# Two adaLN layers on one core: the transposes of the causal values in four halves, and a later start for the rows to be routed

## The chip, the cores and the metric

The kernel runs on one core of a Trainium2 chip. The metric is the device time of one execution in microseconds (us); the time of a kernel is the median of its runs.

## The reference, cut to what matters

32 sequences of 256 tokens with 128 features pass through two layers. Each layer is attention and then a feed-forward part, each behind a layer norm whose scale and shift, and whose gate at the output, come from a small conditioning matrix. Layer 0 has full attention and a feed-forward part quantized to FP4. Layer 1 has causal attention with 16 heads of 8 features, and a mixture of experts of which each token takes two. The part in question is the causal attention:

```python
qkv = jnp.einsum('bse,ef->bsf', inputs, qkv_kernel) + qkv_bias
qkv_heads = qkv.reshape(b, heads, s, -1)
q, k, v = jnp.split(qkv_heads, 3, axis=-1)
qk = jnp.einsum('bhse,bhte->bhst', q, k) / np.sqrt(2.0 * hidden)
mask = jnp.triu(jnp.full((s, s), -jnp.inf, dtype=jnp.float32), k=1)
attn = jax.nn.softmax(qk + mask, axis=-1)
out = jnp.einsum('bhst,bhte->bhse', attn, v).reshape(b, s, e)
...
x = x + ga * out                      # then layer norm, router, two experts a token
```

## The kernel before

The tokens are handled in 16 groups of 512 (two sequences). Three stages follow each other: layer 0 (all groups), the causal stage, and the expert stage, which takes tiles of 256 or 128 rows that share a pair of experts.

**The causal stage** is one long loop. One turn of it is a *unit*; eight units, numbered 0 to 7, are here called a *pass*, and pass g makes the scores of group g. In each unit:

- `maxima` (L852) makes a part of the scores (matmuls of L866 into `c_s`), adds the mask (L873), and VectorE takes the maxima of it (`c_mx`, L877);
- `values` (L943) multiplies the probabilities made two units earlier with the transposed values (`c_po`, L953);
- `probs` (L916) makes scores of 12 units earlier again, transposed (`c_t`, L925); ScalarE takes their exponentials, two instructions of 128x640 (`c_p`, L933), and GpSimd clears what is above the diagonal (L936).

Between these stand the pieces of a table (`put`, L1265): a piece with place n, slot 0 or 1 and a lead is issued in unit n, before (`k` = 0) or after (`k` = 1) `probs`, for the group that is `lead` after the pass's own. The order of instructions on TensorE (PE), VectorE (DVE), ScalarE (ACT) and GpSimd (POOL) is the order of this program text, since the loop stands in `tc.manual_schedule` (L1311). The transfers that SyncE issues (SP) are put in order by a planner.

**The score banks.** `maxima` and `probs` each take two tiles per unit from one pool of three tiles:

```python
ps_s = ph.enter_context(tc.tile_pool(name="c_ps_s", bufs=3, space=PSUM))
```

Each tile is two PSUM banks of 128x512. A tile can be written again only when the engine that reads it is done: DVE for scores (L877), ACT for `c_t` (L933). The matmuls of L866 go to the first tile for two of the four lanes and to the second for the other two, so a unit's first four weight loads on PE belong to the first tile, the other twelve begin with the second.

Two further pieces borrow a tile of this pool: `d_logits` in unit 4 (router logits of an earlier group, `d_pl`, copied out by ACT at L1052 and L1053), and `c_v` (L842). `c_v` transposes the values of half a group with eight matmuls (`c_pv`, L849), and ACT copies all 128x1024 out to `c_vT` (L850). It stands in slot 1 of units 1 and 5.

Other pieces that the prediction speaks of: `c_turn` (unit 7, slot 0) turns the normalized tokens of a later group (`c_xt`), and ACT writes them modulated to `c_hT`; `d_turn` does the same in unit 1 (`d_hT`); `c_norm` and `d_norm` are the ACT instructions of L782. `d_rank` (L1085 to L1090) and `d_count` are steps of the routing on DVE and PE; they run once for a batch of three groups, in passes 7, 10, 13 and 8, 11, 14.

**Maxima back into q.** `place_maxima` (L902, unit 1) writes the maxima of the group before by eight SP transfers (L912) into `c_q`, from which `c_t` is made from unit 4 on.

**Rows to be routed.** `d_start` (L1000, units 2 and 3, lead -3) takes the moments for the second layer norm. In unit 2 it also takes a tile of `rows` from a pool of six, writes the token numbers (GpSimd iota, L1005) and loads the gates (two SP transfers, L1010). `d_keep` (L1015, unit 4, slot 1) copies the residual into the tile. `d_scatter` (L1160) writes the tiles to DRAM by indirect transfers from GpSimd (L1166); a tile of `rows` is free again when they have landed.

Of the kernel before, what the change touches and what calls it, by code (L numbers as in the profile page):

```python
# [10 lines left out]
F32 = mybir.dt.float32  # L11
BF16 = mybir.dt.bfloat16
I32 = mybir.dt.int32
# [6 lines left out]
P = 128  # L20
D = 128
TPG = 4
GT = TPG * P
# [11 lines left out]
def adaln_two_layers(ctx: ExitStack, tc: tile.TileContext, ins, out: bass.AP):  # L35
    nc = tc.nc
# [21 lines left out]
    TOKEN, WEIGHT, RES, GATE, ROW = D, D + 1, D + 3, 2 * D + 3, 3 * D + 3  # L58
# [36 lines left out]
    xg = []  # L95
# [31 lines left out]
    ident = const.tile([P, P], F32, tag="ident", name="ident")  # L127
# [6 lines left out]
    for l in range(2):  # L134
        sc = mp.tile([NB, D], F32, tag=f"sc{l}", name=f"sc{l}")
        nc.scalar.activation(sc, c_sb[l], AF.Silu)
        pt = mps.tile([P, 512], F32, tag="mps", name=f"mps_t{l}")
# [12 lines left out]
        m = const.tile([D, 6, NB], F32, tag=f"mod{l}", name=f"mod{l}")  # L150
# [81 lines left out]
    with ExitStack() as ph:  # L232
# [12 lines left out]
        sb4 = ph.enter_context(tc.tile_pool(name="ab_sb4", bufs=4))  # L245
        ps = ph.enter_context(tc.tile_pool(name="ab_ps", bufs=3, space=PSUM))
        ps_s = ph.enter_context(tc.tile_pool(name="a_ps_s", bufs=2, space=PSUM))
# [395 lines left out]
    r_rows = ctx.enter_context(tc.tile_pool(name="r_rows", bufs=6))  # L643
# [11 lines left out]
    with ExitStack() as ph:  # L655
# [3 lines left out]
        sb4 = ph.enter_context(tc.tile_pool(name="c_sb4", bufs=4))  # L659
        sb5 = ph.enter_context(tc.tile_pool(name="c_sb5", bufs=5))  # L660
        ps = r_ps
        ps_s = ph.enter_context(tc.tile_pool(name="c_ps_s", bufs=3, space=PSUM))
# [21 lines left out]
        for n in range(NP):  # L684
# [5 lines left out]
            pattern=[[1, P]], channel_multiplier=-1,  # L690
# [6 lines left out]
        gates = {}  # L697
# [10 lines left out]
        L = 32  # L708
        HR = L // 2
        B = 64  # L710
        NQ = NPOS // B
# [52 lines left out]
        def moments_half(m, g, tag, h):  # L764

            x = xg[g]
            if h == 0:
                m["mv"] = ln.tile([P, TPG, 2], F32, tag=f"mv{tag}", name=f"mv{tag}{g}")
            st = ln.tile([P, 2, 6], F32, tag=f"st{tag}", name=f"st{tag}{g}_{h}")
            for i in range(2):  # L770
                nc.vector.bn_stats(st[:, i, :], x[:, 2 * h + i, :])
            for i in range(2):
                nc.vector.bn_aggr(m["mv"][:, 2 * h + i, :], st[:, i, :])
            if h == 1:
                m["stats"] = scales(m.pop("mv"), g, tag)
# [63 lines left out]
            for h in range(2):  # L839
                nc.scalar.activation(vx[:, :, h], m["v", j], AF.Copy, scale=half[:, h : h + 1])  # L840

        def c_v(g, j):  # L842

            m = made[g]
            vT = m["vT", j] = sb4.tile([P, 2 * NQ, 4, L], F32, tag="vT", name=f"c_vT{g}_{j}")
            vx = m["vx", j].rearrange("p n h -> p (n h)")
            pt = ps_s.tile([P, 2, 512], F32, tag="s", name=f"c_pv{g}_{j}").rearrange("p e n -> p (e n)")
            for b in range(2 * NQ):
                nc.tensor.transpose(pt[:, b * P : (b + 1) * P], vx[:, b * P : (b + 1) * P], ident)  # L849
            nc.scalar.copy(vT.rearrange("p j l c -> p (j l c)"), pt)  # L850

        def maxima(u):  # L852

# [141 lines left out]
        toward, batch_of = {}, {}  # L995
# [4 lines left out]
        def d_start(g, h):  # L1000
            m = toward.setdefault(g, {})
            moments_half(m, g, "d", h)
            if h == 0:
                rows = m["rows"] = r_rows.tile([P, TPG, ROW], F32, tag="rows", name=f"d_rows{g}")
                nc.gpsimd.iota(  # L1005
                    rows[:, :, TOKEN : TOKEN + 1].bitcast(I32), pattern=[[P, TPG], [0, 1]], base=g * GT,
                    channel_multiplier=1,
                )
                for h in range(2):
                    nc.sync.dma_start(  # L1010
                        rows[:, 2 * h : 2 * h + 2, GATE : GATE + D],
                        gates[5][2 * g + h : 2 * g + h + 1, :].unsqueeze(1).to_broadcast([P, 2, D]),
                    )

        def d_keep(g):  # L1015
            nc.gpsimd.tensor_copy(toward[g]["rows"][:, :, RES : RES + D], xg[g])

        def d_norm(g, h):
            scaled_half(toward[g], g, "d", h)
# [170 lines left out]
        def row_const(name, shape, values):  # L1190
# [11 lines left out]
            number, pattern=[[1, NMOST]], base=0, channel_multiplier=0, allow_small_or_imprecise_dtypes=True  # L1202
# [62 lines left out]
        def put(n, k, lead, piece, *more):  # L1265
            beside[n][k].append((lead, piece, more))
# [5 lines left out]
        for j in range(NB2):  # L1272
            for n, k, piece, more in (
                (5, 0, c_rows, (0,)), (6, 1, c_apart_q, ()), (6, 0, c_rows, (1,)), (9, 1, c_apart_k, (0,)), (10, 1, c_apart_k, (1,)),
                (7, 0, c_rows, (2,)), (8, 1, c_apart_v, ()), (9, 1, c_v, ()),
            ):
                n += 4 * j
                put(n % NU, k, 1 - n // NU, piece, j, *more)
# [4 lines left out]
        for h in range(2):  # L1283
            put(4 + 4 * h if h == 0 else 0, 0, 3 - h, c_start, h)
            put(1 + 2 * h, 1, 2, c_norm, h)
            put(2 + h, 0, -3, d_start, h)
            put(5 + 2 * h, 1, -3, d_norm, h)
        put(4, 1, -3, d_keep)
        put(1, 0, -4, d_turn)
        put(4, 0, -4, d_logits, 0)  # L1290
# [52 lines left out]
    with ExitStack() as ph:  # L1343
# [3 lines left out]
        sb4 = ph.enter_context(tc.tile_pool(name="d_sb4", bufs=4))  # L1347
# [7 lines left out]
        for c in range(NCH):  # L1355
            lo, hi, here = c * P, (c + 1) * P, []
            while lo < hi:
                e = lo // HID1
# [165 lines left out]
```

## Time and profile before

| | |
|---|---|
| three runs | 1520.52, 1524.13 (median), 1525.28 us |
| the profiled execution | 1523.4 us, span 1521.7 us, mean granted TensorE clock 0.969 |
| busy over the span | PE 92%, DVE 65%, ACT 51%, POOL 49% |
| 0 to 415 us, layer 0 | PE busy 342.0 us, clock 0.94 |
| 415 to 467 us, causal stage before and at the first exponentials | PE 46.1 of 52 us, clock 0.85 |
| 467 to 920 us, causal stage, even run | PE 439.6, DVE 370.8, ACT 309.8, POOL 287.0 of 453 us, clock 1.00 |
| 920 to 976 us, its end and the first expert tile | PE 36.9 of 56 us, clock 0.86 |
| 976 to 1522 us, expert tiles | PE 530.5 of 546 us, clock 0.99 |

The views name an instruction by its line and by output and input tile. PE is the matmul itself, PEld its weight load; a row of the timeline is a run of equal instructions (x16) with its start, its length, and in brackets the engine's idle time before it and who ended that. fp32 matmuls appear twice each, so the eight matmuls of one unit's L866 are x16. A busy PE also contains waits within a run of matmuls, so the PEld rows tell more precisely when PE was held.

### The profile page before, as it was taken

To read this page: it belongs to the slowest core of one execution; us is meant where nothing else is said; L and a number is where in the kernel's file an instruction comes from. 1 tells how busy PE (TensorE), PEld (TensorE's weight loads), DVE (VectorE), ACT (ScalarE), POOL (GpSimd) and SP (SyncE) were. 2 spreads that over 40 slices of the span, in tenths; PEclk is the share of its full clock that TensorE was granted. 3 is DMA by queue.
4 is the path that set the end of the run, shared out by engine and by line. 5 is a ranking of instruction groups with operands and counts; after the bars stand their busy time and mean duration, and the time that the engine had idled before them with its cause. 6 is when DMAs were issued, how large, how long until landed. Compare 5 with 4: busy or idle time off the path is not lost.

```text
span 1521.7 us, 33348 instructions
## 1 busy us (share of the span) xinstructions
PE 1395.0 (92%) x12505; PEld 1097.1 (72%) x12505; DVE 995.9 (65%) x2219; ACT 770.7 (51%) x1491; POOL 743.9 (49%) x1079
## 2 busy tenths in 40 slices
PE   5888989988689999999999999598999999999997
PEld 4665666644357677767677676487999999999996
DVE  6799998999487887888887877146333333333332
ACT  5998877843345677667667657241222222222221
POOL 4767866674334555558668577426222222122122
PEclk9999999998799999999999999799999999999999
DMA  8000000000000000001102011866657777777760
GB/s 225 1 1 1 1 1 1 1 1 1 12 2 3 13 17 14 20 6 58 38 26 67 14 44 55 268 178 210 192 170 238 232 218 227 228 216 232 230 188 11
DMA packets 132065, 139.25 MB, mean 92 GB/s; under 512 B 14377, under 2 KB 105969, under 8 KB 131905
## 3 DMA queue, kind: packets, MB, share of 16 engines
q1 hardware_dynamic: 125600, 119.92, 27.1%
q0 software_dynamic: 6304, 17.21, 3.1%
q8 instruction: 99, 1.62, 0.5%
q14 instruction: 62, 0.50, 0.1%
HBM read 116.95 MB, written 19.61 MB: 90 GB/s over the span
## 4 chain that ended last, share of the span: by engine, by line
PE 73%; DVE 16%; ACT 3%; issue 3%; POOL 3%; DMA 1%; SPq 1%; POOLq 0%; DVEq 0%; ACTq 0%
PE d_y L1439 12%; PE d_pg L1453 11%; PE d_pu L1453 11%; PE c_t L925 8%; PE c_s L866 7%; PE c_po L953 5%; PE c_pq L803 3%; PE c_s L873 2%; PE c_pv L849 2%; DVE c_mx L877 2%; PE b_pu L485 2%; DVE qxh L382 2%; DVE sch L378 1%; DVE sch L370 1%; PE b_pg L476 1%
## 5 line engine op out<-in xcount | busy, mean ns | idle before, releaser
L1459 DVE TENSOR_TENSOR d_h<-d_act,d_pu 128x512 f32<-128x512 f32 (+2 forms) x207 | 132.9, 643 | 298.9 <-PE d_pu L1453 273.0
L1457 ACT ACTIVATE d_act<-d_pg 128x512 f32<-128x512 f32 (+2 forms) x207 | 116.2, 561 | 401.7 <-PE d_pg L1453 353.7
L877 DVE TENSOR_REDUCE c_mx<-c_s 128x10 f32<-128x640 f32 x256 | 198.5, 817 | 68.5 <-PE c_s L873 67.3
L933 ACT ACTIVATE c_p<-c_t 128x640 f32<-128x640 f32 x256 | 166.1, 701 | 120.2 <-PE c_t L925 116.9
L1439 PE MATMUL d_y<-d_wd,d_h 128*128 128x128 f32 (+1 forms) x1656 | 209.4, 281 | 5.5 <-DVE d_h L1459 2.9
L1439 PEld LDWEIGHTS d_y<-d_wd,d_h 128*128 128x128 f32 (+1 forms) x1656 | 198.7, 191 | 20.9 <-DVE d_h L1459 7.0
L1453 PE MATMUL d_pg<-d_sT,d_wg 128*128 128x256 f32 (+1 forms) x924 | 204.3, 348 | 1.2 <-DMA d_wg<-in_L_ffn_w_dram 1.2
L1453 PE MATMUL d_pu<-d_sT,d_wu 128*128 128x256 f32 (+1 forms) x924 | 200.9, 344 | 0.5 <-DMA d_wu<-in_L_ffn_w_dram 0.5
L936 POOL TENSOR_SCALAR_AFFINE_SELECT c_p<-c_p 128x256 f32<-128x256 f32 x256 | 111.4, 442 | 145.7 <-ACT c_p L933 144.3
L1453 PEld LDWEIGHTS d_pu<-d_sT,d_wu 128*128 128x128 f32 x924 | 154.6, 192 | 17.0 <-DMA d_wu<-in_L_ffn_w_dram 1.2
L866 PEld LDWEIGHTS c_s<-c_k,c_qx 32*128 32x128 f32 x2048 | 106.7, 188 | 68.3 <-issue 24.0
L866 PE MATMUL c_s<-c_k,c_qx 32*128 32x256 f32 (+3 forms) x2048 | 141.5, 335 | 12.1 <-ACT c_p L933 8.8
L1453 PEld LDWEIGHTS d_pg<-d_sT,d_wg 128*128 128x128 f32 x924 | 142.1, 193 | 13.0 <-DVE d_sT L1422 1.6
L1478 POOL TENSOR_TENSOR d_o<-d_o,d_slot 128x256 f32<-128x256 f32 (+1 forms) x42 | 25.3, 604 | 244.7 <-DVE d_o L1477 234.8
L925 PE MATMUL c_t<-c_q,c_kx 32*128 32x128 f32 (+3 forms) x2048 | 139.2, 332 | 4.3 <-DVE c_mx L877 3.4
L1481 POOL DMA_INDIRECT out_dram<-d_o,d_slot x69 | 68.5, 993 | 141.5 <-DMA out_dram<-d_o,d_slot 129.0
L925 PEld LDWEIGHTS c_t<-c_q,c_kx 32*128 32x128 f32 x2048 | 111.3, 185 | 28.7 <-DVE c_mx L877 9.1
L953 PE MATMUL c_po<-c_p,c_vT 128*32 128x256 f32 (+3 forms) x2048 | 99.0, 307 | 6.8 <-POOL c_p L936 5.7
L834 POOL TENSOR_SCALAR c_kx<-c_k,half 128x512 f32<-128x512 f32 x64 | 102.4, 1602 | 1.1 <-DVE c_k L819 1.1
L953 PEld LDWEIGHTS c_po<-c_p,c_vT 128*32 128x32 f32 x2048 | 54.6, 109 | 37.0 <-POOL c_p L936 7.6
L485 PE MATMUL b_pu<-wupT,b_hqT 128*128 128x352 f32 x128 | 55.6, 519 | 19.6 <-DVE b_hh L491 19.6
L1166 POOL DMA_INDIRECT slots<-d_rows,d_index x64 | 64.5, 1008 | 16.3 <-issue 15.2
(301 smaller groups left out, 2566.7 us busy)
## 6 DMA issues: line engine op xcount, KB each, us to landing
d_wg<-in_L_ffn_w_dram SPq DMA_DIRECT2D x84, 352.0 KB, 3.5
d_wu<-in_L_ffn_w_dram SPq DMA_DIRECT2D x84, 352.0 KB, 5.3
d_wd<-in_L_ffn_w_dram SPq DMA_DIRECT2D x84, 320.0 KB, 6.2
d_slot<-slots SPq DMA_DIRECT2D x27, 387.0 KB, 3.2
x<-in_L_attn_X_dram SPq DMA_DIRECT2D x16, 256.0 KB, 5.7
d_rows<-gates SPq DMA_DIRECT2D x32, 128.0 KB, 4.7
d_slot<-slots SPq DMA_DIRECT2D x15, 193.5 KB
d_wd<-in_L_ffn_w_dram SPq DMA_DIRECT2D x84, 32.0 KB, 5.8
```

Source lines behind the costliest of these rows:

```text
L485: nc.tensor.matmul(pu[:, :HID0], lhsT=hT[:, i * P : (i + 1) * P], rhs=wT["up"], start=True, stop=True)
L834: nc.gpsimd.tensor_scalar(m["kx", j][:, :, h], m["k", j], half[:, h : h + 1], None, ALU.mult)
L866: nc.tensor.matmul(s[lane // 2][:, lane % 2, at : at + w], lhsT=qx[rows, NQ * e + b, :, :].rearrange("p h n -> p (h n)"), rhs=k[rows, e * ...
L877: nc.vector.tensor_reduce(mx[:, n, 2 * x : 2 * x + 2, :], s[x][:, :, 0:W].rearrange("p l (b n) -> p l b n", n=B), AX.X, ALU.max, negate=True,)
L925: nc.tensor.matmul(s[lane // 2][:, lane % 2, at : at + w], lhsT=kx[rows, (NQ * e + b) * P : (NQ * e + b + 1) * P], rhs=q[rows, (e + 1) * N ...
L933: nc.scalar.activation(t[:, :, 0:W], s[x][:, :, 0:W], AF.Exp, scale=SCALE1)
L936: nc.gpsimd.affine_select(out=diagonal, in_=diagonal, compare_op=ALU.is_ge, fill=0.0, base=1, pattern=[[0, 4], [2, B]] if sub else [[0, 2] ...
L953: nc.tensor.matmul(po[rows, (e + 1) * NPOS - w : (e + 1) * NPOS], lhsT=v[:, NQ * e + b, lane, :], rhs=p[lane // 2][:, lane % 2, at : at + ...
L1439: nc.tensor.matmul(y[k][:, b, :], lhsT=h[r0:r1, j, b * P : (b + 1) * P], rhs=wd[r0:r1, c, :], start=first and b == 0, stop=last and b == N ...
L1453: nc.tensor.matmul(to[:, j, :], lhsT=w[:, c * P : (c + 1) * P], rhs=hT, start=True, stop=True)
L1457: nc.scalar.activation(act[:, :m, :], pg[:, :m, :], AF.Silu)
L1459: nc.vector.tensor_tensor(h[:, :m, :], act[:, :m, :], pu[:, :m, :], ALU.mult)
```

## The change

`c_v` is called four times instead of two: with `e` 0 and 1 for each half of a group, in slot 1 of units 1, 3, 5 and 7. Each call takes a tile of the score banks, uses one of its two banks for four transposes, and ACT copies 128x512 of it. The tile of `rows`, its iota and its two gate transfers move from `d_start` (unit 2) to `d_keep` (unit 4).

```diff
-        def c_v(g, j):
+        def c_v(g, j, e):
             m = made[g]
-            vT = m["vT", j] = sb4.tile([P, 2 * NQ, 4, L], F32, tag="vT", name=f"c_vT{g}_{j}")
+            if e == 0:
+                m["vT", j] = sb4.tile([P, 2 * NQ, 4, L], F32, tag="vT", name=f"c_vT{g}_{j}")
             vx = m["vx", j].rearrange("p n h -> p (n h)")
-            pt = ps_s.tile([P, 2, 512], F32, tag="s", name=f"c_pv{g}_{j}").rearrange("p e n -> p (e n)")
-            for b in range(2 * NQ):
-                nc.tensor.transpose(pt[:, b * P : (b + 1) * P], vx[:, b * P : (b + 1) * P], ident)
-            nc.scalar.copy(vT.rearrange("p j l c -> p (j l c)"), pt)
+            pt = ps_s.tile([P, 2, 512], F32, tag="s", name=f"c_pv{g}_{j}_{e}")[:, 0, :]
+            for b in range(NQ):
+                at = (NQ * e + b) * P
+                nc.tensor.transpose(pt[:, b * P : (b + 1) * P], vx[:, at : at + P], ident)
+            nc.scalar.copy(m["vT", j][:, NQ * e : NQ * (e + 1), :, :].rearrange("p j l c -> p (j l c)"), pt)
...
         def d_start(g, h):
             m = toward.setdefault(g, {})
             moments_half(m, g, "d", h)
-            if h == 0:
-                rows = m["rows"] = r_rows.tile([P, TPG, ROW], F32, tag="rows", name=f"d_rows{g}")
-                nc.gpsimd.iota(
...
-                for h in range(2):
-                    nc.sync.dma_start(
...
         def d_keep(g):
-            nc.gpsimd.tensor_copy(toward[g]["rows"][:, :, RES : RES + D], xg[g])
+            m = toward[g]
+            rows = m["rows"] = r_rows.tile([P, TPG, ROW], F32, tag="rows", name=f"d_rows{g}")
+            nc.gpsimd.iota(
...
+            for h in range(2):
+                nc.sync.dma_start(
...
+            nc.gpsimd.tensor_copy(rows[:, :, RES : RES + D], xg[g])
...
-                (7, 0, c_rows, (2,)), (8, 1, c_apart_v, ()), (9, 1, c_v, ()),
+                (7, 0, c_rows, (2,)), (8, 1, c_apart_v, ()), (9, 1, c_v, (0,)), (11, 1, c_v, (1,)),
```

More of the change, by code (lines that the diff above doesn't have):

```diff
@@ L1002, in d_start, with d_keep @@
             moments_half(m, g, "d", h)
-            if h == 0:
-                rows = m["rows"] = r_rows.tile([P, TPG, ROW], F32, tag="rows", name=f"d_rows{g}")
-                nc.gpsimd.iota(
-                    rows[:, :, TOKEN : TOKEN + 1].bitcast(I32), pattern=[[P, TPG], [0, 1]], base=g * GT,
-                    channel_multiplier=1,
-                )
-                for h in range(2):
[L1010 to L1015, printed above, removed]
-            nc.gpsimd.tensor_copy(toward[g]["rows"][:, :, RES : RES + D], xg[g])
+        def d_keep(g):
+            m = toward[g]
+            rows = m["rows"] = r_rows.tile([P, TPG, ROW], F32, tag="rows", name=f"d_rows{g}")
+            nc.gpsimd.iota(
+                rows[:, :, TOKEN : TOKEN + 1].bitcast(I32), pattern=[[P, TPG], [0, 1]], base=g * GT,
+                channel_multiplier=1,
+            )
+            for h in range(2):
+                nc.sync.dma_start(
+                    rows[:, 2 * h : 2 * h + 2, GATE : GATE + D],
+                    gates[5][2 * g + h : 2 * g + h + 1, :].unsqueeze(1).to_broadcast([P, 2, D]),
+                )
+            nc.gpsimd.tensor_copy(rows[:, :, RES : RES + D], xg[g])
         def d_norm(g, h):
```

## The prediction

> **What bounds the kernel now.** I read the page's chain first, then the busy time by stages, then who waits for the exponentials, and last the timeline at the ends of odd units. From the page:
>
> ```profile
> span 1521.7 us, 33348 instructions
> ...
> PE 73%; DVE 16%; ACT 3%; issue 3%; POOL 3%; DMA 1%; SPq 1%; POOLq 0%; DVEq 0%; ACTq 0%
> ```
>
> Three quarters of the chain that ends last are PE. The busy times by stage say how full PE is in the even run of the causal stage:
>
> ```profile
> 467.00:920.00 453.00, 439.62 (x6350) 320.53 (x6350) 370.80 (x799) 309.83 (x535) 286.97 (x467) 1.00 0.10 28
> ```
>
> The first two sums are PE and PEld: 439.6 of 453 us, at clock 1.00. So what keeps PE back here costs time, and ACT with 309.8 us has room. The view of line L933 in that window says who waits for the exponentials, and what they wait for (us, times):
>
> ```profile
>   PE c_t L925: 99.1, 81
> ...
>   PEld c_s L866: 20.5, 31
> ```
>
> ACT waits for PE's `c_t`, and PE's scores `c_s` for ACT: a loop over the three score tiles. The timeline shows how it closes. End of unit 3, pass 9, with no `c_pv`:
>
> ```profile
> 708.35 0.82 PEld L925 LDWEIGHTS c_t<-c_q,c_kx 32*128 32x128 f32 x16 [0.20 <-ACT c_qx L826]
> ...
> 709.28 1.30 ACT L933 ACTIVATE c_p<-c_t 128x640 f32<-128x640 f32 x2 [0.98 <-PE c_t L925]
> ...
> 709.34 0.33 PEld L866 LDWEIGHTS c_s<-c_k,c_qx 32*128 32x128 f32 x4 [0.17 <-issue]
> ...
> 710.03 0.73 PEld L866 LDWEIGHTS c_s<-c_k,c_qx 32*128 32x128 f32 x12 [0.37 <-issue]
> ```
>
> The next unit's scores begin at once in their first tile (x4). The second (x12) starts at 710.03, 0.05 after the *first* exponential ends (709.28 + 0.70, the mean of one): with three tiles in turn, that tile is the one of the first `c_t`. End of unit 5, where `c_pv` stands:
>
> ```profile
> 717.36 1.30 ACT L933 ACTIVATE c_p<-c_t 128x640 f32<-128x640 f32 x2 [0.83 <-PE c_t L925]
> 717.41 0.85 PEld L849 LDWEIGHTS c_pv<-ident,c_vx 128*128 128x128 f32 x8 [0.17 <-issue]
> ...
> 718.44 1.00 PEld L866 LDWEIGHTS c_s<-c_k,c_qx 32*128 32x128 f32 x16 [0.17 <-issue]
> ```
>
> `c_pv` has taken a tile, so the turn is one further: the first scores need the first exponential's tile (free at 718.06), the second scores the *second* one's (717.36 + 1.30 = 718.66). The x16 take 1.00 and end at 719.44, which is 718.66 + 0.05 + 0.73. So the second exponential already sets the end here; the eight transposes only fill the time before it. Unit 1 is the same (second exponential to 702.89, plus 0.05 and 0.73 is 703.67, the end of `c_s`). And the end of unit 7, without `c_pv`, where ACT is late because `c_hT` goes first:
>
> ```profile
> 693.17 0.31 PEld L866 LDWEIGHTS c_s<-c_k,c_qx 32*128 32x128 f32 x4
> ...
> 693.65 1.30 ACT L933 ACTIVATE c_p<-c_t 128x640 f32<-128x640 f32 x2
> ...
> 694.40 0.73 PEld L866 LDWEIGHTS c_s<-c_k,c_qx 32*128 32x128 f32 x12 [0.93 <-ACT c_p L933]
> ```
>
> Again the x12 follow the first exponential (693.65 + 0.70 = 694.35).
>
> **The change part by part.**
>
> *Units 1 and 5 lose four transposes each: 0.* Four of the eight weight loads are 0.43 us, but the second exponential sets the end; without them PE merely idles before it. After the change `c_s` still ends at 703.67 and 719.44 in the pass shown.
>
> *Units 3 and 7 gain a `c_pv`: +0.60 at each end.* The borrowed tile moves the turn by one, so the x12 wait for the second exponential instead of the first: 1.30 less 0.70, that is 0.60 later. Unit 3: 710.63 for 710.03; unit 7: 695.00 for 694.40. The four transposes themselves (0.17 + 0.43) cost nothing, since PE waits there now (0.37 and 0.93 idle) and waits longer afterwards.
>
> How often: exponentials run in unit 3 of passes 2 to 15 and, with scores to follow, in unit 7 of passes 1 to 14: 28 ends, 28 x 0.60 = 16.8. Does later work swallow any? DVE and ACT mostly wait for PE, so a delay of `c_s` moves them along. In two places it does not. In passes 7, 10 and 13 `d_rank` occupies DVE after unit 3:
>
> ```profile
> 645.10 1.55 DVE L877 TENSOR_REDUCE c_mx<-c_s 128x10 f32<-128x640 f32 x2
> ...
> 646.70 0.80 PEld L925 LDWEIGHTS c_t<-c_q,c_kx 32*128 32x128 f32 x12 [0.36 <-DVE c_mx L877]
> ```
>
> The reduces start about 1.1 us after their scores stood ready (PE went on to `c_po` at 644.00), so 0.60 goes in there: -1.8 for three passes. And in pass 12 `c_t` of unit 4 is held for `c_q`:
>
> ```profile
> 803.71 0.88 SPq L1010 DMA_DIRECT2D d_rows<-gates  x2
> ...
> 804.75 6.60 SPq L912 DMA_DIRECT2D c_q<-c_mT  x8
> ...
> 812.95 1.08 PEld L925 LDWEIGHTS c_t<-c_q,c_kx 32*128 32x128 f32 x12 [0.29 <-issue]
> ```
>
> In pass 9 the x16 of this place took 0.74; here they started at 812.19 and end at 814.03, 1.1 late. 0.60 of delay fits in: -0.6. Left: 24 x 0.60 = 14.4.
>
> *The start of the stage.* In passes 0 and 1 before unit 4 of pass 1 there are no exponentials; there the extra tile makes the second scores wait for the second maximum instead of the first, 0.73 later, at three ends. DVE is nearly full there, so 0 to 2.2; I take 1.2, as DVE's own lateness swallows about 0.3 each time.
>
> *ACT.* 64 copies of 128x512 for 32 of 128x1024: the nearest row, L1053's 128x512 out of the same banks, takes 0.59, the old copy 1.01, so 32 x 0.17 = 5.4 us more. It lies beside the 99.1 us in which ACT waits for `c_t`; in units 3 and 7 only `xn` (0.87) follows, and the next exponential is over 2 us away. Cost 0; without that cover 5.4.
>
> [...]
>
> *The rows, two units later.* The iota (0.15 each on POOL) and the two gate transfers (0.9 on SP) move from unit 2 to unit 4; nothing reads them before the scatters, two passes on. On SP they move past nothing with a near deadline but the eight transfers of `c_mT`, which in passes 9 and 12 stood behind them while they waited for scatters to land (12 such waits, 50.5 us, in SP's view of waits). If they now stand behind, pass 12 loses its 1.1, of which 0.6 was counted already as swallowing: -0.5. If the planner leaves the order, 0, as the landing they wait for is no later. The end on the other side is +1.1, one more pass held like pass 12. I take 0, the middle.
>
> *Sum.* 14.4 + 1.2 = 15.6 on the profiled execution's 1523.4 us (1.7 of it lie around the span): 1539.0. That execution is 0.7 below the median of 1524.13, within the runs' spread of 4.8, so I leave it at **1539 us**.
>
> **The rivals.** A measurement of this kernel tells about 0.3%, 4.6 us, from no change.
>
> *Faster: the turn of the tiles doesn't bind.* If tiles were handed out so that the scores after `c_pv` needed no later exponential than before, units 1 and 5 would lose 0.43 each, units 3 and 7 would take their halves into the idle 0.37 and 0.93: about 0.8 a pass, 14 passes, 11 us, 1512. It decides if the x16 of unit 5 end before the second exponential; for it speaks nothing in the rows, against it the 719.44 worked out above. 0.06.
>
> *No change.* The exponentials' lateness is made up later in the pass, as in pass 7, in most passes: under 0.15 us is left of each 0.60. Against it: in pass 9 every later wait of PE is tied to PE's own progress. 0.06.
>
> *Much slower: the clock.* The granted clock was 1.00 from 467 to 920 although PE waits at the end of units. With more waits it could drop as it did at 415 to 467 (0.85 in the mean, of 52 us: 8 us lost). If two such stretches were added, 16 us more, 1555. It decides if PE's short waits join up; the longest stays near 0.9 us, so 0.07.
>
> [...]
>
> **How the numbers follow.** The forecast with its own unknowns (start 0 to 2.2, rows -0.5 to 1.1, some further swallowing of up to a quarter of 14.4, and the clock at both ends of the stage, worth a few us from run to run: the three runs differ by 4.8) reaches from 1530 (10.8 and 0 and -0.5, less 3.5 for the clock) to 1547 (14.4, 2.2 and 1.1, 0.7 for the median, and 5 for the clock) and has 0.81. Beyond lie the rivals with 0.19. Slower by over 0.3%: 0.81 and 0.07; same 0.06; faster 0.06.
>
> **What would show it right or wrong.** Right: in units 3 and 7 the timeline shows `c_pv` x4, then `c_s` whose last twelve loads start 0.05 after the second exponential; ends of units 1 and 5 unmoved, with idle PE after four transposes; passes 3 to 6 longer by 1.2 us; the copies near 0.59; PE's idle time for L933 up by some 15 us or more. Wrong: the scores after `c_pv` starting before the second exponential's end; passes that are no longer than before; a clock below 1.00 between 467 and 920 us.

## The result: 1539.1 us, and the profile after

The changed kernel took 1539.12 us in the median of seven runs (1533.31 to 1545.12), the kernel before 1523.16 us on the same chip (1520.41 to 1525.28). The ratio is 1.0105, with a 95% interval of 1.0082 to 1.0129: slower by 1.05%, and clear of 1. The forecast was 1539.0, within 1530 to 1547, and slower with a chance of 0.88. The size agrees more closely than its terms do; that is taken apart below.

The profiled execution after the change took 1536.1 us, with a clock of 0.963. From its page, the span and the engines' shares of the chain that ended last:

```profile
span 1534.4 us, 33354 instructions
...
PE 74%; DVE 13%; ACT 5%; issue 3%; POOL 2%; SPq 1%; DMA 1%; POOLq 0%; DVEq 0%; ACTq 0%
```

ACT's share of the chain has gone from 3% to 5%. The page's list of lines puts 2% of it down to `c_p`, that is, to the exponentials. The busy times by stage (PE, PEld, DVE, ACT and POOL, then clock, DMA share and GB/s):

```profile
467.00:932.00 465.00, 452.48 (x6332) 320.64 (x6332) 368.93 (x797) 308.94 (x560) 287.20 (x466) 1.00 0.10 27
```

The even run is 12 us longer. PEld, DVE, ACT and POOL are within 2 us of what they were in the 453 us before. Apart from ACT's copies (38.0 us of them in the whole execution, 32.4 before) the engines do the same work; it takes longer because PE is held. (The sum for PE itself, 452.48 for 439.62 with PEld at 320.64 for 320.53, contains waits within runs of matmuls.) The clock stayed at 1.00. Who waits around the exponentials, from the view of their line L935 between 467 and 930 us:

```profile
  PE c_t L927: 110.6, 81
...
  PEld c_s L868: 39.5, 116
```

The prediction's figures of this view (99.1 and 20.5 us) belong to 476 to 920 us, which leaves out the first 9 us of the stretch that it named. From 467 to 920 us the view of before has:

```profile
  PE c_t L925: 101.4, 82
...
  PEld c_s L866: 21.4, 32
```

So PE's score loads wait 116 times for an exponential where they waited 32 times, 39.5 us in all for 21.4: 18 us more, where the prediction said 15 or more. ACT's own waits for `c_t` grew by 9.2 us. The timeline shows the mechanism. End of unit 3 in pass 9, where the new `c_pv` stands:

```profile
715.10 0.82 PEld L927 LDWEIGHTS c_t<-c_q,c_kx 32*128 32x128 f32 x16 [0.20 <-ACT c_qx L826]
...
716.04 1.30 ACT L935 ACTIVATE c_p<-c_t 128x640 f32<-128x640 f32 x2 [0.98 <-PE c_t L927]
716.04 0.42 PEld L851 LDWEIGHTS c_pv<-ident,c_vx 128*128 128x128 f32 x4
...
716.79 0.30 PEld L868 LDWEIGHTS c_s<-c_k,c_qx 32*128 32x128 f32 x4 [0.33 <-ACT c_p L935]
...
717.22 0.59 ACT L852 COPY c_vT<-c_pv 128x512 f32<-128x512 f32 x1
717.39 0.73 PEld L868 LDWEIGHTS c_s<-c_k,c_qx 32*128 32x128 f32 x12 [0.29 <-ACT c_p L935]
```

The first four score loads wait for the first exponential (716.04 + 0.70 = 716.74, and 0.05). The other twelve start at 717.39, 0.05 after the second one ends (716.04 + 1.30). From the start of `c_t` to the end of `c_s` it is 3.02 us (715.10 to 718.12); before it was 2.41 (708.35 to 710.76). The copy of 0.59 begins only at 717.22, when the exponentials are done, and the scores do not wait for it. End of unit 5, from which four transposes were taken:

```profile
723.78 0.82 PEld L927 LDWEIGHTS c_t<-c_q,c_kx 32*128 32x128 f32 x16 [0.20 <-issue]
...
724.71 1.30 ACT L935 ACTIVATE c_p<-c_t 128x640 f32<-128x640 f32 x2 [0.82 <-PE c_t L927]
724.77 0.42 PEld L851 LDWEIGHTS c_pv<-ident,c_vx 128*128 128x128 f32 x4 [0.17 <-issue]
...
725.47 0.30 PEld L868 LDWEIGHTS c_s<-c_k,c_qx 32*128 32x128 f32 x4 [0.28 <-ACT c_p L935]
...
726.06 0.73 PEld L868 LDWEIGHTS c_s<-c_k,c_qx 32*128 32x128 f32 x12 [0.29 <-ACT c_p L935]
```

From the start of `c_t` to the end of `c_s` it is 3.01 us (723.78 to 726.79), and it was 3.01 before (716.43 to 719.44). The transposes removed here left idle PE in their place. And the end of unit 7 in the same timeline:

```profile
699.55 0.42 PEld L851 LDWEIGHTS c_pv<-ident,c_vx 128*128 128x128 f32 x4
...
699.82 1.29 ACT L935 ACTIVATE c_p<-c_t 128x640 f32<-128x640 f32 x2
...
701.16 0.73 PEld L868 LDWEIGHTS c_s<-c_k,c_qx 32*128 32x128 f32 x12 [0.29 <-ACT c_p L935]
```

From the first exponential to the end of `c_s` it is 2.07 us (699.82 to 701.89); before it was 1.48 (693.65 to 695.13).

It is so throughout: in every pass from 2 to 14 the twelve loads behind units 1, 3, 5 and 7 start 0.05 after the second exponential's end. Before, those behind units 3 and 7 started 0.05 after the first one's.

The passes of both executions, each from its first score load to that of the next pass (pass 9 of before: 693.17 to 725.25, of after: 700.57 to 733.84):

| pass | before, us | after, us | change |
|---|---|---|---|
| 0 and 1 | 51.71 | 52.69 | +0.98 |
| 2, 3 | 31.17 each | 32.54, 32.35 | +1.37, +1.18 |
| 4, 6, 9 | 32.08 each | 33.27 each | +1.19 each |
| 5 | 32.08 | 33.55 | +1.47 |
| 7, 10, 13 | 34.15 to 34.18 | 34.90 | +0.73 each |
| 8, 11, 14 | 33.00 to 33.07 | 33.77, 34.05, 33.78 | +0.77, +1.05, +0.71 |
| 12 | 33.11 | 33.26 | +0.15 |
| 15, to its unit 7 | 28.16 | 28.17 | 0 |

A plain pass (4, 6, 9) is longer by 1.19, which is twice the 0.60 of the second exponential. In passes 5 and 11 some 0.28 on top is not the borrow's: e6 below, which borrows as many tiles as before, is longer by 0.27 and 0.28 there.

The cut at the first load distorts the ends of the table. Behind unit 7 the first four loads now wait as well, so unit 7 is longer by 1.23 (2.90 to 4.13) and the next unit 0 shorter by 0.64 (4.99 to 4.35). In the middle of the table the two belong together. But the row of passes 0 and 1 has some 0.6 too much by it, which is missing in the rows of 14 and 15. Cut at the *end* of unit 0's scores instead, passes 0 and 1 are longer by 0.35, passes 2 to 14 by 13.0 in all (pass 14 by 1.24), and pass 15, to the end of its scores, by 0.1.

### The profile page after: what moved, and what is told of

It reads as the page before. It is cut to its first block, busy times and chain, and to the rows that moved or that the text cites. A ratio compares the mean times of both kernels' runs of the same rounds, so it can differ in the third digit from the quotient of the medians.

```text
span 1534.4 us, 33354 instructions
## 1 busy us (share of the span) xinstructions
PE 1410.0 (92%) x12505; PEld 1099.9 (72%) x12505; DVE 993.5 (65%) x2219; ACT 772.5 (50%) x1523; POOL 742.1 (48%) x1079
## 4 chain that ended last, share of the span: by engine, by line
PE 74%; DVE 13%; ACT 5%; issue 3%; POOL 2%; SPq 1%; DMA 1%; POOLq 0%; DVEq 0%; ACTq 0%
PE d_y L1441 12%; PE d_pg L1455 11%; PE d_pu L1455 11%; PE c_s L868 9%; PE c_t L927 7%; PE c_po L955 5%; PE c_pq L803 3%; PE c_s L875 2%; DVE qxh L382 2%; PE b_pu L485 2%; ACT c_p L935 2%; DVE c_mx L879 1%; DVE sch L370 1%; PE c_pv L851 1%; PE b_py L527 1%
## 5 line engine op out<-in xcount | busy, mean ns | idle before, releaser
L935 ACT ACTIVATE c_p<-c_t 128x640 f32<-128x640 f32 x256 | 166.1, 701 | 131.6 <-PE c_t L927 126.5
L868 PE MATMUL c_s<-c_k,c_qx 32*128 32x256 f32 (+3 forms) x2048 | 148.6, 339 | 13.2 <-ACT c_p L935 6.9
L927 PE MATMUL c_t<-c_q,c_kx 32*128 32x128 f32 (+3 forms) x2048 | 135.9, 333 | 4.1 <-DVE c_mx L879 3.8
L1168 POOL DMA_INDIRECT slots<-d_rows,d_index x64 | 64.7, 1010 | 16.7 <-issue 12.7
```

The source lines that it names most:

```text
L868: nc.tensor.matmul(s[lane // 2][:, lane % 2, at : at + w], lhsT=qx[rows, NQ * e + b, :, :].rearrange("p h n -> p (h n)"), rhs=k[rows, e * ...
L927: nc.tensor.matmul(s[lane // 2][:, lane % 2, at : at + w], lhsT=kx[rows, (NQ * e + b) * P : (NQ * e + b + 1) * P], rhs=q[rows, (e + 1) * N ...
L935: nc.scalar.activation(t[:, :, 0:W], s[x][:, :, 0:W], AF.Exp, scale=SCALE1)
```

## The experiments

Theory A, that of the prediction: what costs time is the *number of tiles borrowed from the score banks*. Each borrowed tile moves the turn on by one, so that the next scores wait for the second exponential instead of the first. Rival B: the place of the values, or their transposes and copies, costs the time. Rival C: the rows do. Each table row compares with the kernel before on the same chip; the chips differ (before had medians of 1522.77, 1521.52 and 1531.62), so only ratios are compared across them. The ratios are the recorded ones; they can differ from the quotient of the two medians by 0.001. Plain passes are 4 and 6; pass 9 is the same but in e4 (32.26) and e8 (31.53).

| kernel | median us | before there | ratio, 95% interval | plain pass, us |
|---|---|---|---|---|
| e1_rows | 1521.62 | 1522.77 | 0.9993, 0.9983 to 1.0003 | 32.08 |
| e2_halves | 1539.77 | 1522.77 | 1.0113, 1.0095 to 1.0131 | 33.27 |
| e3_other_bank | 1508.77 | 1522.77 | 0.9917, 0.99 to 0.9934 | 30.90 |
| e4_whole_late | 1516.80 | 1522.77 | 0.9961, 0.9946 to 0.9976 | 32.08 |
| e5_empty | 1538.44 | 1521.52 | 1.0110, 1.0093 to 1.0127 | 33.27 |
| e6_two_copies | 1519.76 | 1521.52 | 0.9994, 0.9984 to 1.0003 | 32.08 |
| e7_count_later | 1501.25 | 1521.52 | 0.9872, 0.9857 to 0.9886 | 30.90 |
| e8_count_tables | 1510.53 | 1531.62 | 0.9869, 0.9852 to 0.9885 | 30.90 |

### The two parts apart: e1_rows and e2_halves

e1 is the kernel before with the rows taken in `d_keep`, values as they were:

```diff
         def d_start(g, h):
...
-            if h == 0:
-                rows = m["rows"] = r_rows.tile(...)
...
         def d_keep(g):
-            nc.gpsimd.tensor_copy(toward[g]["rows"][:, :, RES : RES + D], xg[g])
+            m = toward[g]
+            rows = m["rows"] = r_rows.tile(...)
+            nc.gpsimd.iota(
...
+            nc.gpsimd.tensor_copy(rows[:, :, RES : RES + D], xg[g])
```

> The kernel before with only the rows to be routed (tile, iota, gate transfers) moved to unit 4. Theory (the tile turn makes the loss): 0 to -2.5 us against before, that is 1521 to 1524: in the profile of the change pass 8 is only 0.77 longer and there the cast d_index took 0.17 instead of 0.59 us, because the copy of the residual no longer stands beside it; pass 12 may keep its late c_t (6.35 us for unit 4). Rival (the moved transfers and the later copy cost): +5 us or more, and passes 3 to 6 longer than 32.08 us.

e2 is the other part alone, `c_v` in halves and its four places:

```diff
-        def c_v(g, j):
+        def c_v(g, j, e):
...
-                (7, 0, c_rows, (2,)), (8, 1, c_apart_v, ()), (9, 1, c_v, ()),
+                (7, 0, c_rows, (2,)), (8, 1, c_apart_v, ()), (9, 1, c_v, (0,)), (11, 1, c_v, (1,)),
```

> The kernel before with only the four half transposes in units 1, 3, 5, 7. Theory: the whole loss, +14 to +18 us (1537 to 1541), passes 3 to 6 at 33.3 us as in the changed kernel, second part of the scores 0.05 us after the second exponential in all four odd units. Rival (the rows carry it): under +8 us.

Measured: 1.0113 for the halves alone and 0.9993 for the rows alone, the latter's interval reaching past 1. The halves carry the whole loss, and rival C falls. In e2 the twelve loads start 0.05 after the second exponential behind all four odd units of passes 2 to 14, as expected. The rows' part is a gain of about 1 us, if anything (1522.77 to 1521.62). The passes say where it may come from: 8 and 11 are 0.42 shorter each than before. In those two passes the cast `d_index` (DVE) had started inside a copy of POOL; in the kernel before:

```profile
683.13 0.60 POOL L1016 COPY d_rows<-x 128x512 f32<-128x512 f32 x1
683.17 0.59 DVE L1153 CAST d_index<-d_where 128x12 uint32<-128x12 f32 x1
```

and in e1, where an iota stands ahead of the copy and the cast comes first:

```profile
682.99 0.17 DVE L1153 CAST d_index<-d_where 128x12 uint32<-128x12 f32 x1
683.07 0.60 POOL L1016 COPY d_rows<-x 128x512 f32<-128x512 f32 x1
```

The cast took 0.59 instead of 0.17, which is the 0.42 of the pass. Pass 11 shows the same pair (0.60, then 0.17). In pass 14 the cast came only near the copy's end (in before 0.53 after its start, taking 0.17), so there was nothing to gain, and e1 gained nothing there. Passes 7, 10 and 13 became 0.1 longer and pass 12 0.45 shorter; I did not follow those, but pass 12 differs between executions anyway (e6, without the moved rows, is 0.92 shorter there). On SP the planner kept its order: gates first, then the transfers of `c_mT`.

### The borrow without its work: e5_empty

The values stand whole in units 1 and 5, as before. In units 3 and 7 a tile of the score banks is taken, one transpose of 8 columns goes into it, and ACT copies 8x8 out. Nothing reads the copy:

```diff
+        def c_borrow(g, j):
+            pt = ps_s.tile([P, 2, 512], F32, tag="s", name=f"c_pb{g}_{j}")
+            nc.tensor.transpose(pt[:8, 0, 0:P], ident[:, 0:8], ident)
+            bit = sb2.tile([8, 8], F32, tag="bit", name=f"c_bit{g}_{j}")
+            nc.scalar.copy(bit, pt[:8, 0, 0:8])
...
-                (7, 0, c_rows, (2,)), (8, 1, c_apart_v, ()), (9, 1, c_v, ()),
+                (7, 0, c_rows, (2,)), (8, 1, c_apart_v, ()), (9, 1, c_v, ()), (11, 1, c_borrow, ()),
```

> The kernel before, unchanged in its two whole transposes, with two more borrowings of a score tile that do next to nothing: in units 3 and 7 one transpose of eight columns goes into a tile of the pool and ScalarE copies 8x8 of it. It adds 32 of each and leaves nothing out. Theory: four tiles are borrowed per pass as in the changed kernel, so passes 3 to 6 take 33.3 us (32.08 plus two times 0.60) and the whole is 1536 to 1541. Rival (the moved transposes and copies cost, not the turn of the tiles): at most 32 small instructions of 0.2 us on either engine, 1524 to 1529.

Measured: 1.0110, and a plain pass of 33.27, to a hundredth the one of the halves. Its timeline at the end of unit 3 (its lines stand five or more further down):

```profile
715.46 1.30 ACT L940 ACTIVATE c_p<-c_t 128x640 f32<-128x640 f32 x2 [0.98 <-PE c_t L932]
715.47 0.08 PEld L855 LDWEIGHTS c_pb<-ident 128*8 128x8 f32 x1
...
716.22 0.30 PEld L873 LDWEIGHTS c_s<-c_k,c_qx 32*128 32x128 f32 x4 [0.66 <-issue]
...
716.65 0.14 ACT L857 COPY c_bit<-c_pb 8x8 f32<-8x8 f32 x1
...
716.81 0.73 PEld L873 LDWEIGHTS c_s<-c_k,c_qx 32*128 32x128 f32 x12 [0.29 <-ACT c_bit L857]
```

One weight load of 0.08 holds the place of the four transposes. PE then sits idle for 0.66, and the twelve loads still start at 716.81, which is 715.46 + 1.30 + 0.05. The view puts this wait down to the copy `c_bit` (716.65 to 716.79), which happens to end beside the second exponential (716.76). By the turn, though, the twelve loads write the tile that the second exponential reads, while `c_bit` reads the borrowed one; and with the real `c_pv`, whose copy only began when the exponentials were done, they started the same 0.05 after the exponential. The transposes and their copy are not what costs; the tile is.

### The copy alone, and the place alone: e6_two_copies and e4_whole_late

e6 keeps one tile and eight transposes and only copies it out in two instructions:

```diff
-            nc.scalar.copy(vT.rearrange("p j l c -> p (j l c)"), pt)
+            for e in range(2):
+                nc.scalar.copy(
+                    vT[:, NQ * e : NQ * (e + 1), :, :].rearrange("p j l c -> p (j l c)"), pt[:, e * 512 : (e + 1) * 512]
+                )
```

> The kernel before with each copy of the transposed values (128x1024, 1.01 us) made as two of 128x512, from the same borrowed tile in units 1 and 5. Theory: 32 more instructions on ScalarE, about 5 us of its time, all beside its waits for c_t: within 1.5 us of before, passes 3 to 6 at 32.08. Rival (more instructions on ScalarE cost): +5 us or more.

e4 keeps the whole `c_v`, in units 3 and 7 instead of 1 and 5:

```diff
-                (7, 0, c_rows, (2,)), (8, 1, c_apart_v, ()), (9, 1, c_v, ()),
+                (7, 0, c_rows, (2,)), (8, 1, c_apart_v, ()), (11, 1, c_v, ()),
```

> The kernel before with its two whole calls of c_v (eight transposes, one copy) in units 3 and 7 instead of 1 and 5. Theory: a borrowed tile costs one exponential (0.60) wherever it stands, and two are still borrowed: units 1 and 5 end 0.6 earlier, units 3 and 7 0.6 later, in sum 1519 to 1527. Rival (units 3 and 7 are the wrong place for transposes, since ScalarE is late there): +8 us or more.

Measured: two copies change nothing (0.9994 with an interval that reaches past 1, plain pass 32.08; the median is 1.8 us lower, just outside the 1.5 expected). With the place moved, the plain pass is 32.08 too: two borrows, the same length, wherever they stand. So B falls for the plain passes. Yet e4 was faster than expected (0.9961). In the profiled execution the causal stage's scores take 5.4 us less, and not in the plain passes: 7, 10 and 13 are shorter by 0.55 each, 12 by 0.8, the start of the stage and pass 15 by 1.5 each. (Its span is only 2.2 us shorter, as what follows the scores took 3.3 us longer; this execution lies 4.5 us above e4's median.) The expectation overlooked that a borrow costs less where its delay is swallowed. In passes 7, 10 and 13 two more borrows add only 0.59 to 0.63 in e2 and e5, so one of the two is all but free there, and e4 has one in that place. Behind unit 7 of pass 15 no scores follow, so that a borrow there costs nothing: cut at the ends of the scores, pass 15 of e4 is shorter by 0.60 behind each of units 1 and 5 and longer by 0.59 behind unit 3. That agrees with theory A, though no run moves one of these borrows alone. Pass 12 and the start differ between executions by as much (pass 12: 0.92 shorter in e6), so they tell nothing here.

### No borrow at all: e3_other_bank

The changed kernel, with the halves put into the one bank (pool `ps`) in which `c_turn`, `d_turn`, `d_count` and others have their results. The tile of `d_logits` stays in the score banks, here as in all these kernels:

```diff
-            pt = ps_s.tile([P, 2, 512], F32, tag="s", name=f"c_pv{g}_{j}_{e}")[:, 0, :]
+            pt = ps.tile([P, 512], F32, tag="ps", name=f"c_pv{g}_{j}_{e}")
```

> The changed kernel with the four half transposes written to the one bank of the pool that the projections use, so that no score tile is borrowed at all. Theory: the loss goes and a little more: in units 1 and 5 the scores end 0.4 us earlier than before the change, in units 3 and 7 some 0.2 to 0.3 later, in passes 8, 11 and 14 the transposes of unit 3 wait for d_count's bank, 1 us or so: 1517 to 1523 in all. Rival (twice as many calls, 32 more copies on ScalarE, split transposes cost by themselves): stays at 1535 to 1541, since all of that work is still there.

Measured: 0.9917, with its interval below 1, better than expected. Its timeline at the end of unit 3, pass 5:

```profile
568.97 1.30 ACT L935 ACTIVATE c_p<-c_t 128x640 f32<-128x640 f32 x2 [0.98 <-PE c_t L927]
568.98 0.42 PEld L851 LDWEIGHTS c_pv<-ident,c_vx 128*128 128x128 f32 x4
...
569.56 0.89 PEld L868 LDWEIGHTS c_s<-c_k,c_qx 32*128 32x128 f32 x16 [0.17 <-issue]
```

The scores run without a stop, all sixteen together, though the second exponential ends only at 570.27. The second scores are back in the first exponential's tile, free at 569.67. The view of L935 from 467 to 905 us says the same of the whole run:

```profile
  PE c_t L927: 87.9, 82
...
  PEld c_s L868: 3.2, 6
```

Six waits of 3.2 us are left of 116 of 39.5 us. The plain pass is 30.90, so the three sizes stand in a row: 30.90, 32.08 and 33.27 us for 0, 2 and 4 tiles borrowed for the values, 0.59 to 0.60 for each. That is theory A, measured from both sides. My expectation had counted the transposes in units 3 and 7 as a cost of 0.2 to 0.3 each and too little for units 1 and 5. In fact units 3 and 4 of a plain pass together take 8.01 where before took 8.02: PE's idle time there takes the transposes in wholly.

Passes 8 and 14 of e3 were longer than before instead (34.17 and 34.12). In unit 3 `c_pv` now waits for the bank that `d_count` has filled and that DVE reads late (pass 8):

```profile
665.45 0.23 DVE L1142 TENSOR_TENSOR d_at<-d_pn,nxt 128x78 f32<-128x78 f32 x1
...
665.73 0.42 PEld L851 LDWEIGHTS c_pv<-ident,c_vx 128*128 128x128 f32 x4 [1.65 <-DVE d_at L1142]
```

### The last wait removed: e7_count_later and e8_count_tables

e7 is e3 with `d_count` one unit later. It makes its last tables before the last count, so not all of its expert tiles are the right ones, and it speaks for the causal stage alone. In e8 the last tables follow the count:

```diff
-            (0, 1, -6, d_pair, 1), (1, 1, -6, d_pair, 2), (3, 0, -6, d_count), (4, 1, -6, d_place),
+            (0, 1, -6, d_pair, 1), (1, 1, -6, d_pair, 2), (4, 0, -6, d_count), (4, 1, -6, d_place),
...
-            put(3, 1, -6, lambda g, kind: tables(kind) if g == NG - 1 else False, kind)
+            put(4, 1, -6, lambda g, kind: tables(kind) if g == NG - 1 else False, kind)
```

> The kernel of e3_other_bank with the counting step d_count moved from unit 3 to unit 4 (slot 0), so that the transposes of unit 3 no longer wait for its bank. Passes without it are 30.9 us there and stay so. Theory: passes 8, 11 and 14 come down from 34.2, 32.9 and 34.1 to about 31.9 (30.9 and the 0.9 that they were longer than others in the kernel before), 3 to 6 us in all, 1503 to 1506. Rival (those passes are long because of the routing's VectorE work itself): 1508 to 1510, no change.

> As e7_count_later, with the tables of the expert tiles also one unit later, behind the last count (in e7_count_later the last tables were made before it, so its expert tiles were not all the right ones). Theory: the causal stage as in e7_count_later, and the whole within 3 us of it: 1499 to 1505. Rival (e7_count_later owed its time to its wrong tables): 1508 or more, as e3_other_bank.

Measured: passes 8, 11 and 14 fall to between 31.3 and 31.6 us in both, a little below the 31.9 expected; the ratios are 0.9872 and 0.9869. The absolute time expected of e8 was missed because its chip was slower (before took 1531.62 there); the ratio is that of e7. e8 is the fastest version that makes its tables from all counts: 1.3% below the kernel before, and 2.3% below the changed kernel by the two ratios (0.9869 / 1.0105 = 0.977).

## Why the prediction was right, step by step

**Units 1 and 5: 0.** Confirmed; from `c_t` to the end of `c_s` unit 5 takes 3.01 us before and after, unit 1 3.16.

**Units 3 and 7: 0.60 each.** Confirmed in place and size: +0.61 and +0.59 in the rows above, +1.19 in the plain passes, and the experiments show that it is the tile alone (e5), in proportion to the number of tiles (e3, e4, e2).

**What later work swallows.** Passes 7, 10 and 13 swallow 0.47 each in the changed kernel, but that contains the rows: without these, in e2 and e5, it is 0.56 to 0.60 each, the forecast's 0.60 (e1, the rows alone, is longer there by 0.11 to 0.14). Pass 12 came to 33.26, the length of a plain pass, so all of its 1.1 of lateness is gone, 1.04 instead of 0.6. As this lateness varies between executions (e6 has next to none of it with as many borrows as before), what the borrows swallowed of it is open. What the prediction overlooked stands behind unit 7 of pass 14: 0.48 is swallowed there. Before the change the twelve later loads of `c_t` in the next unit waited 0.38 for the maxima (until 895.95); after it `c_t` does not wait for them (907.12). That is not the rows' doing: e2 and e5 show it too (pass 14: 33.74 and 33.72). Unit 3 of pass 15 costs its 0.59.

**Start of the stage.** Cut at the ends of the scores, passes 0 and 1 are longer by 0.35, where the forecast had 1.8 (1.2, and 0.6 for unit 7 of pass 1). One execution each can't settle this term: e2 and e5, with as many borrows, came to +1.5 and -0.5.

**ACT copies: 0.** Confirmed: the median of one copy is 0.593 after the change, 5.6 us more in all, and e6, which only splits the copies (0.592), has the ratio 0.9994. The cover of 99.1 us that the term names is that of 476 to 920 us; from 467 on it is 101.4.

**Rows: 0.** Off by about 1 us (1.15 between e1's medians, though its interval reaches past 1). The term only looked at SP's queue, where the order stayed; that the gates stand ahead of `c_mT` in pass 15 too (901.74 and 902.79 in before), the prediction left out. What moved was POOL's copy, behind an iota, and with it the cast on DVE (0.42 in each of two passes).

**Sum.** In the two profiled executions the scores of the stage, from the first load to the end of the last, took 13.4 us longer, where the forecast had 15.6: 0.35 for 1.8 in passes 0 and 1, 13.0 for 13.2 in passes 2 to 14, 0.1 for 0.6 in pass 15. Within the 13.0 errors cancel: the rows took 0.84 off passes 8 and 11, and pass 12 came out 0.44 shorter than forecast; against that, passes 7, 10 and 13 swallowed 0.4 less in all, and passes 5 and 11 had their 0.28 each. The first scores began 1.5 earlier in the execution after, and what follows pass 15 took 0.75 longer, which makes up the spans' 12.7. The medians lie 16.0 apart, though. So the nearness of 1539.0 to 1539.12 is in part an accident: the terms came to about 2 us less, and the execution profiled after lies 3 us below its own median. The seven runs after the change spread over 12 us, those before over 5. What makes the difference outside the passes is open: the granted clock was lower at both ends of the stage (0.84 for 0.85 in 415 to 467 us, and 0.82 in 932 to 988 us for 0.86 in 920 to 976 us, behind the even run), but no run here takes that apart.

**The rivals.** *Faster by a free turn* did not come, since the turn binds; e3 shows what it is worth when the borrow is really gone: 13 to 14 us (by the ratio and by the medians), where 11 were worked out for this rival. The steps differ (1.18 a plain pass for 0.8, less what passes 8, 11 and 14 lose to another bank), so that the two are near each other is luck. *No change* is refuted by the plain passes. *The clock*: it stayed at 1.00 in the even run with its 116 waits, the longest of PEld for an exponential being 0.78 us, and the longest for anything 1.19 (for `c_mx`). That more waits, or waits that join up, would lower it was the author's estimate, and these rows do not show it; e3 has a low clock within the even run, behind two gaps of 1.65 us (last section). Smaller instructions alone gained nothing: e6 makes two copies of 0.592 of each one of 1.013, without a further borrow, and has the ratio 0.9994.

## What to carry to other kernels

Where a pool of tiles is handed out in turn, count the borrowers between two users of it: a borrowed tile costs whatever the next user waits longer, here 0.60 us, even if the borrower itself does nothing. To split a small step into halves doubles its borrows. So put such steps into a bank outside the rotation, then look for the reader that keeps *that* bank late, and move it: here these two steps gave 0.8% and then 0.5% more.

## What the runs showed of the hardware

*Behind one gap the clock was low twice in three times.* In e3 the same gap of 1.65 us between PE's weight loads stood in passes 8, 11 and 14. After that of pass 8, the windows (columns as above) show a low clock:

```profile
467.00:667.00 200.00, 194.56 (x2920) 143.00 (x2918) 170.57 (x361) 143.16 (x259) 118.53 (x195) 1.00 0.06 14
667.00:671.00 4.00, 4.00 (x44) 3.03 (x40) 2.16 (x6) 1.00 (x5) 1.74 (x10) 0.57 0.01 4
```

In pass 14 it was 0.64 (861 to 865 us), and in pass 11 it stayed at 1.00 (765 to 769 us). The kernels before and after the change, whose longest gaps between weight loads are 1.07 and 1.19 us there, show 1.00 from 467 to 905 us, as e8 does. So the clock was low behind two of three such gaps; the gap's length alone does not decide, and what does, no run shows. Unit 4 took 6.14 and 6.00 us in passes 8 and 14, and 4.57 in pass 11. So of the 2.9 us by which pass 8 fell between e3 and e7, some 1.6 (an estimate, 6.14 less 4.57) lie in the unit with the low clock, behind the wait; the eight loads of `d_pl` in it took 1.82 us in pass 8 and 0.97 in pass 11.

*A cast beside a copy.* The cast of 0.17 us took 0.59 when it began within a POOL copy of 0.60, and ended with it (683.76 and 683.73). In pass 11 the cast took 0.60 in the same way (782.41, the copy from 782.38). In pass 14 of e1 it began 0.41 into the copy and took 0.22, to 882.22, where the copy ended at 882.19. Where it began first, it took 0.17, and the copy, which began 0.08 later, was no longer for it (0.60). Why the cast took longer beside the copy, no run shows.
